# A delta-rule attention block between two expert layers: five stages woven group by group in lockstep, or over all groups by due times

## The chip, the core and the metric

The kernel runs on one core of a Trainium2 chip, as one launch. The metric is device microseconds of that core. TensorE (PE) multiplies, VectorE (DVE), ScalarE (ACT) and GpSimd (POOL) do the elementwise work, SyncE (SP) issues the plain transfers, POOL the gathers and scatters.

## The reference

The input is `x`, 4 sequences of 2048 tokens, 256 wide, float32. The block is a macaron: half an expert layer, attention, half an expert layer, each added to `x`.

```python
x = x + 0.5 * ffn(layernorm(x))      # 8 experts, top 2, capacity 1280 tokens each
x = x + attn(layernorm(x))
x = x + 0.5 * ffn(layernorm(x))
# ffn: silu(xg @ wg) * (xg @ wu) @ wd per expert, F = 1024, weighted scatter-add
# attn, 8 heads of 32:
h = rmsnorm(x, ln1_w)
q, k = l2norm(silu(h @ qw)), l2norm(silu(h @ kw));  v = silu(h @ vw)
beta = sigmoid(h @ bw);  g = -exp(A_log) * softplus(h @ aw + dt_bias)
# for every token:  Sg = exp(g) * S;  S = Sg + beta * k (v - k Sg)^T;  o = q S
o = rmsnorm(o, onorm_w) * silu(h @ gw)
x1 = x + 0.5 * (o @ ow)
y = x1 + 0.5 * silu(rmsnorm(x1, ln2_w) @ fcw) @ pw
```

## The kernel before

Three parts follow one another: the first normalisation, routing and the eight experts; attention; routing and the eight experts again. All matmuls of the expert layers and projections are float32, which the profile counts as two passes each.

Attention treats the token recurrence in chunks of C = 32 tokens. One tile holds the same chunk of the B = 4 sequences, 4 x 32 = 128 partitions, so what is done per head and sequence is a 32 x 32 matmul on one quadrant (`by_sequence`, L566). GC = 4 chunks make a group, and there are NG = 16 groups. A group passes through five stages, each a Python generator that yields after every few instructions a pair (time on PE, latency until it can go on) and a flag for small matmuls:

- `stage_load`: fetch the rows `xt`, layer norm statistics.
- `stage_proj`: normalise (`hh`), transpose (`hT`), project to k, q, v and gate (`pp`, 512 wide) and to beta and g (`pb`).
- `stage_prep`: decay factors (`gg`, `gm`, `pe`, `pd`, `eG`, `ed`), norms of k and q, the products of keys and queries (`pgk`), from them the matrix `A` and `KP`; then `X`, the inverse of a unit triangular matrix of 32 x 32 for each head and token block, by 30 steps of two dependent DVE instructions (`tm`, then `X`, L775 and L779); its transpose `XT`; and `pW`, which needs both `XT` and keys multiplied by their decay (`kq` by `eG`, on POOL, L795).
- `stage_chain`: the recurrence over the four chunks: `pc` from `XT` and v, from `WQD` and the state `S`, then, after the transpose `Z`, from `KP` and `Z`; new `S` and output `O` are transposed out by DVE.
- `stage_out`: norm of `O` (`os`, `ro`), transpose, output projection (`ppo`), first residual `x1`, then the feed-forward (`pm_`, `mT`, `py`), the store, the last layer norm `xn` and the router's logits (`pl`).

The order of PE is written out by hand: `weave` takes the stages' generators and emits, at a planned time, the step that is ready and least far along, with turns between small and large matmuls. The other engines' orders are made by the scheduler, from the order of emission and a few priorities (`urgent`). All engines execute their queues in order. In the version before, `weave` is called 20 times; round `it` holds output of group `it`, chain of `it`+1, preparation of `it`+2, projection of `it`+3 and loading of `it`+4, and every step of a round is emitted before any of the next:

```python
stages = ((65, stage_out), (24, stage_chain), (68, stage_prep), (68, stage_proj), (60, stage_load))
for it in range(1 - len(stages), NG):
    weave([(n, stage, it + d) for d, (n, stage) in enumerate(stages) if 0 <= it + d < NG])
```

The pools `p1` to `p6` have as many buffers as their names say; the PSUM pools `pj` (projections), `tpp` (transposes), `mp` (preparation) and `chp` (chain) have two banks each.

Of the kernel before, what the change touches and what calls it, by code (L numbers as in the profile page):

```python
# [9 lines left out]
F32 = mybir.dt.float32  # L10
# [3 lines left out]
ALU = mybir.AluOpType  # L14
# [4 lines left out]
P = 128  # L19
# [15 lines left out]
for _n, _w in (  # L35
    ("ident", P), ("blk", P), ("before", P), ("after", P), ("upto", P),
    ("prior", P), ("total", P), ("iota", P), ("mle", C),
    ("eye", C), ("below", C), ("rev8", E),
):
    _COLS[_n] = (_W, _W + _w)  # L40
    _W += _w
_PLACE = _W
# [6 lines left out]
def constants():  # L49

    p = np.arange(P)
    b, t = p // C, p % C
    same = b[:, None] == b[None, :]
    c = {
        "ident": np.eye(P),
        "blk": same,
        "before": same & (t[:, None] < t[None, :]),
        "after": same & (t[:, None] > t[None, :]),
        "upto": same & (t[:, None] <= t[None, :]),
        "prior": (b[:, None] < b[None, :]) & (t[:, None] == 0),  # L60
        "total": np.broadcast_to(t[:, None] == 0, (P, P)),
        "iota": np.broadcast_to(p[None, :], (P, P)),
        "mle": t[:, None] <= np.arange(C)[None, :],
        "eye": t[:, None] == np.arange(C)[None, :],
        "below": -30000.0 * (t[:, None] > np.arange(C)[None, :]),
        "rev8": np.broadcast_to(E - np.arange(E)[None, :], (P, E)),
    }
    out = np.zeros((P, _FIND + _FINDS), np.float32)
    for n, (lo, hi) in _COLS.items():
        out[:, lo:hi] = c[n]  # L70
    ch = np.arange(_PLACES)[None, :]
    for i, row in enumerate((p[:, None] * _PLACES + ch, b[:, None] * C * _PLACES + C * ch + t[:, None])):
        lo = _PLACE + 2 * i * _PLACES
        out[:, lo : lo + _PLACES] = row // P
        out[:, lo + _PLACES : lo + 2 * _PLACES] = row % P


    k = P // E
    steps = [k << b for b in range(28, -1, -2) for k in range(4)]
    find = (  # L80
        p[:, None] // k == p[None, :] // k, p[:, None] < p[None, :], p[:, None] == k * np.arange(E),
        np.broadcast_to(np.array(steps, np.int32).view(np.float32), (P, _STEPS)),
    )
    out[:, _FIND:] = np.concatenate(find, axis=1)
    return out
# [10 lines left out]
def macaron_kernel(  # L96
# [19 lines left out]
    cst = cpool.tile([P, _W], F32, name="cst")  # L116
    nc.sync.dma_start(out=cst, in_=consts[:, :_W])
    K = {n: cst[:, lo:hi] for n, (lo, hi) in _COLS.items()}
# [4 lines left out]
    nc.vector.tensor_copy(before16, K["before"])  # L123
    nc.vector.tensor_copy(blk16, K["blk"])
    nc.vector.tensor_copy(iota16, K["iota"])
    ident16 = cpool.tile([P, P], BF16, name="ident16")
    below16 = cpool.tile([P, C], BF16, name="below16")
    nc.vector.tensor_copy(ident16, K["ident"])
    nc.vector.tensor_copy(below16, K["below"])

# [377 lines left out]
    def attention(x1_d, logits, xn_d, x2_d):  # L508
# [4 lines left out]
        with ExitStack() as st:  # L513
# [5 lines left out]
            pv = pool("v", 10)  # L519
# [81 lines left out]
            def stage_load(g):  # L601
# [4 lines left out]
                yield 0, 40  # L606
                for c in range(GC):
                    stats(xt, c, mv)
                    yield 0, 4
# [12 lines left out]
            def stage_proj(g):  # L622
# [5 lines left out]
                yield 0, 40  # L628
                for c in range(GC):
                    hh = p2.tile([P, D], F32, tag="hh", name="hh")  # L630
# [4 lines left out]
                    hT = p2.tile([P, 2, P], F32, tag="hT", name="hT")  # L635
# [21 lines left out]
            def stage_prep(g):  # L657
# [109 lines left out]
                for c in range(GC):  # L767
                    nc.gpsimd.tensor_tensor(
                        KP[:, c, :, 1, :], kq[:, c, 0], bc(edc[:, c, :, C - 1], [2], [P, H, C]), ALU.mult
                    )  # L770
                for j in range(1, C - 1):
# [10 lines left out]
                nc.gpsimd.memset(X[:, 0 : C * C : C + 1], 1.0)  # L782
                for c in range(GC):
                    nc.gpsimd.tensor_tensor(
                        WQD[:, c, :, 2, :], bc(K["eye"], [1], [P, H, C]), bc(eG[:, 1, c], [2], [P, H, C]), ALU.mult
                    )
# [6 lines left out]
                for c in range(GC):  # L793
                    for j in range(2):
                        nc.gpsimd.tensor_tensor(kq[:, c, j], kq[:, c, j], bc(eG[:, 0, c], [2], [P, H, HD]), ALU.mult)  # L795
                    nc.vector.transpose(WQD[:, c, :, 1, :], kq[:, c, 1])
                    yield 0, 0.5
# [8 lines left out]
            def stage_chain(g):  # L806
# [3 lines left out]
                O = G["O"] = p2.tile([P, GC, H, HD], F32, tag="O", name="O")  # L810
                os_ = G["os"] = p2.tile([P, GC, H], F32, tag="os", name="os_")
                for c in range(GC):
# [15 lines left out]
                    for f in range(2):  # L828
# [5 lines left out]
                        nc.vector.transpose(O[:, c, f * HH : (f + 1) * HH], pc[f][:, :, 1])  # L834
# [6 lines left out]

            def stage_out(g):
                G = live[g]
                xt, r, nm, O, os_ = (G[n] for n in ("xt", "r", "nm", "O", "os"))

# [8 lines left out]
                x1 = p1.tile([P, GC, D], F32, tag="x1", name="x1")  # L854
                sx = p2.tile([P, GC], F32, tag="sx", name="sx")
                for c in range(GC):
                    shd = [P, H, HD]
                    nc.vector.tensor_tensor(O[:, c], O[:, c], bc(ro[:, c], [2], shd), ALU.mult)
                    oT = p2.tile([P, 2, P], F32, tag="hT", name="oT")
# [5 lines left out]
                    pp = pj.tile([P, D], F32, tag="pj", name="ppo")  # L865
# [8 lines left out]

                nc.vector.tensor_scalar(sx, sx, 1.0 / D, RMS_EPS, ALU.mult, ALU.add)
# [6 lines left out]
                for c0 in range(0, GC, 2):  # L882
                    hT2 = p2.tile([P, 2, 2 * P], F32, tag="hT2", name="hT2")
                    for i in range(2):
                        c = c0 + i
                        hh = p2.tile([P, D], F32, tag="hh2", name="hh2")
# [40 lines left out]
                xn = p1.tile([P, GC, D], F32, tag="x1", name="xn")  # L927
                for c in range(GC):
# [3 lines left out]
                    xnT = p2.tile([P, 2, P], F32, tag="hT", name="xnT")  # L932
# [12 lines left out]
            def weave(streams):  # L945
# [7 lines left out]
                todo = []  # L953
                for n, stage, g in streams:
                    known = plans.get(stage)
                    todo.append([0.0, 0.0, n, stage(g), known, plans.setdefault(stage, []), 0])
                while todo:
                    ready = [t for t in todo if t[0] <= now]
                    if not ready:
                        now = min(t[0] for t in todo)  # L960
                        continue
                    turn = small if now - since < (1.6 if small else 3.2) else not small

                    def rank(t):
                        coming = t[4][t[6]] if t[4] and t[6] < len(t[4]) else (0, 0)
                        return bool(coming[0]) and (len(coming) > 2) != turn, t[1]

                    t = min(ready, key=rank)
                    step = next(t[3], None)
                    if step is None:  # L970
                        todo.remove(t)
                        continue
# [7 lines left out]
                    t[0] = now + step[1]  # L980
                    t[1] += (step[0] + step[1]) / t[2]
# [4 lines left out]
            stages = ((65, stage_out), (24, stage_chain), (68, stage_prep), (68, stage_proj), (60, stage_load))  # L986
            for it in range(1 - len(stages), NG):
                with tc.manual_schedule(engines={mybir.EngineType.PE}):
                    weave([(n, stage, it + d) for d, (n, stage) in enumerate(stages) if 0 <= it + d < NG])
# [57 lines left out]
```

## Time and profile before

| | us |
|---|---|
| median of 3 runs (3786.07 to 3793.11) | 3789.86 |
| the profiled execution | 3772.04 |
| its span | 3770.3 |
| first matmul of attention | 1162.8 |
| start of the first `pW` of group 0, 4, 13, 15 | 1237.6, 1588.7, 2414.0, 2590.0 |
| last logits of attention | 2730.4 |

The profile is one execution. PE's share of busy time counts pipelined matmuls, so it also counts slow ones; the granted clock (1.00 is full) stands beside it. In the timeline a bracket behind a line is the time the engine idled before it, with what released it: "<-DVE O L834" means that DVE's instruction on line 834, which writes `O`, came last; "issue" that nothing in the profile was waited for. In the windows the columns are the length, then for each engine busy time and instructions, then the clock, the share of the DMA engines and GB/s.

### The profile page before, as it was taken

The page shows a single profiled execution, that of the slowest core. Times are in us where ns is not written, and L with a number is a line of the kernel's source. Part 1 is how long each engine was busy: PE and PEld are TensorE (multiplying, and loading weights), DVE is VectorE, ACT ScalarE, POOL GpSimd, SP SyncE. Part 2 cuts the span into 40 slices and gives each one's busy share as a digit, 9 for nine tenths or more (in the row PEclk, how much of TensorE's full clock was granted, in tenths as well). Part 3 has the DMA queues.
Part 4 walks back from the last instruction along what each step waited for, and adds up shares of the span by engine and source line. Part 5 has one row for each costly group of instructions (what it writes and reads, how often), then busy time and mean ns, then how long its engine had stood idle before and what let it go on. Part 6 is the DMA issues. An engine that isn't in the chain of part 4 may idle for free.

```text
span 3770.3 us, 74243 instructions
## 1 busy us (share of the span) xinstructions
PE 3221.2 (85%) x31883; PEld 2262.2 (60%) x31883; DVE 1721.8 (46%) x5216; ACT 854.4 (23%) x1900; POOL 777.8 (21%) x792
## 2 busy tenths in 40 slices
PE   7179998999995588999999999898708999999998
PEld 6146665665663466666677666667504666656666
DVE  6753323211115657666766666665184342221111
ACT  3011111111112233333333333332201111111111
POOL 0033313222211111111121222220003332222211
PEclk6579999999998799999999999998758999999999
DMA  6212211222102000000000000000121222122211
GB/s 244 105 26 56 59 41 31 61 59 59 23 12 68 2 19 19 19 19 19 19 19 19 19 19 19 13 14 13 25 72 26 60 58 53 20 56 62 58 21 14
DMA packets 94873, 152.91 MB, mean 41 GB/s; under 512 B 13257, under 2 KB 77521, under 8 KB 91473
## 3 DMA queue, kind: packets, MB, share of 16 engines
q1 hardware_dynamic: 63824, 106.21, 8.7%
q0 software_dynamic: 30720, 41.96, 6.6%
q8 instruction: 250, 4.10, 0.4%
q14 instruction: 79, 0.64, 0.1%
HBM read 93.09 MB, written 55.05 MB: 39 GB/s over the span
## 4 chain that ended last, share of the span: by engine, by line
PE 76%; DVE 14%; POOL 4%; DMA 3%; issue 2%; ACT 1%; SPq 0%; POOLq 0%; DVEq 0%; ACTq 0%
PE pg L488 15%; PE pu L490 15%; PE po L497 15%; PE pc L566 5%; PE pp L642 5%; PE py L907 5%; PE ppo L867 2%; PE tp L587 2%; DVE oa L451 2%; DVE over L326 2%; POOL kq L795 1%; PE pgk L566 1%; DVE X L779 1%; DVE tm L775 1%; DMA xg<-xn,idx 1%
## 5 line engine op out<-in xcount | busy, mean ns | idle before, releaser
L493 DVE TENSOR_TENSOR hT<-sg,pu 128x512 f32<-128x512 f32 (+1 forms) x384 | 229.4, 599 | 1181.5 <-PE pu L490 1179.6
L488 PE MATMUL pg<-xT,wg_e 128*128 128x512 f32 (+1 forms) x1536 | 637.7, 537 | 0.0
L490 PE MATMUL pu<-xT,wu_e 128*128 128x512 f32 (+1 forms) x1536 | 616.7, 522 | 0.0
L497 PE MATMUL po<-wd_e,hT 128*128 128x256 f32 x2560 | 560.4, 379 | 0.0
L497 PEld LDWEIGHTS po<-wd_e,hT 128*128 128x128 f32 x2560 | 486.4, 190 | 79.8 <-issue 15.3
L488 PEld LDWEIGHTS pg<-xT,wg_e 128*128 128x128 f32 x1536 | 295.4, 196 | 231.2 <-issue 217.1
L490 PEld LDWEIGHTS pu<-xT,wu_e 128*128 128x128 f32 x1536 | 289.4, 191 | 236.1 <-issue 221.9
L492 ACT ACTIVATE sg<-pg 128x512 f32<-128x512 f32 (+1 forms) x384 | 202.0, 526 | 996.3 <-PE pg L488 964.7
L469 POOL DMA_INDIRECT xg<-xn,idx x160 | 248.0, 1550 | 274.7 <-DVE ws L463 183.3
L642 PE MATMUL pp<-wk,hT 128*128 128x512 f32 x512 | 255.3, 618 | 6.7 <-ACT hT L589 6.0
L503 POOL DMA_INDIRECT x_d<-eo,idx x80 | 128.7, 1608 | 636.0 <-ACT eo L502 493.6
L503 POOL DMA_INDIRECT out_dram<-eo,idx x80 | 124.4, 1554 | 637.7 <-ACT eo L502 490.4
L907 PE MATMUL py<-wpj,mT 128*128 128x256 f32 x1024 | 237.4, 380 | 0.0
L907 PEld LDWEIGHTS py<-wpj,mT 128*128 128x128 f32 x1024 | 192.5, 190 | 40.6 <-issue 17.2
L502 ACT ACTIVATE eo<-po,ws 128x256 f32<-128x256 f32 x160 | 75.9, 475 | 542.9 <-PE po L497 542.9
L775 DVE TENSOR_TENSOR tm<-X 128x30 f32<-128x30 f32 (+14 forms) x480 | 157.9, 329 | 10.1
L779 DVE TENSOR_TENSOR X<-X,tm 128x30 f32<-128x30 f32 (+14 forms) x480 | 157.8, 329 | 10.3
L879 POOL TENSOR_TENSOR xt<-xt,x 128x256 f32<-128x256 f32 x64 | 47.2, 738 | 490.0 <-DVE qa L683 376.8
L476 DVE COPY xT<-tpx 128x256 f32<-128x256 f32 x160 | 67.7, 423 | 172.5 <-PE tpx L475 148.1
L451 DVE TENSOR_TENSOR oa<-aM,iota 128x4096 bf16<-128x4096 bf16 x32 | 141.4, 4420 | 4.5 <-PE tpx L475 4.3
L475 PE MATMUL tpx<-cst,xg 128*128 128x128 f32 x320 | 75.0, 322 | 76.1 <-DMA xg<-xn,idx 42.4
L566 PE MATMUL pc<-XT,vg 32*32 32x32 f32 x4096 | 65.4, 211 | 85.4 <-DVE O L834 61.0
(725 smaller groups left out, 4141.0 us busy)
## 6 DMA issues: line engine op xcount, KB each, us to landing
wg_e<-in_L_ffn_wg_dram SPq DMA_DIRECT2D x16, 1024.0 KB, 4.9
wu_e<-in_L_ffn_wu_dram SPq DMA_DIRECT2D x16, 1024.0 KB, 6.6
wd_e<-in_L_ffn_wd_dram SPq DMA_DIRECT2D x16, 1024.0 KB, 5.7
xt_in<-in_L_attn_x_dram SPq DMA_DIRECT2D x8, 1024.0 KB, 7.6
x_d<-xt_in SPq DMA_DIRECT2D x8, 1024.0 KB, 6.4
xn<-in_xn SPq DMA_DIRECT2D x8, 1024.0 KB, 3.9
xt<-x_d SPq DMA_DIRECT2D x64, 128.0 KB, 3.9
out_dram<-xt SPq DMA_DIRECT2D x64, 128.0 KB, 2.3
```

Of the source, the lines that this page charges most:

```text
L451: nc.vector.tensor_tensor(oa, bc(aM[:, e, hf * HC : (hf + 1) * HC], [2], [P, HC, P]), bc(iota16, [1], [P, HC, P]), ALU.is_equal,)
L469: nc.gpsimd.indirect_dma_start(out=xg, out_offset=None, in_=xn_d[:], in_offset=bass.IndirectOffsetOnAxis(ap=idx[:, t : t + 1], axis=0),)
L488: nc.tensor.matmul(pg[:, :n], wg_e[:, k, fs], xT[:, k, cols], start=(k == 0), stop=(k == 1))
L490: nc.tensor.matmul(pu[:, :n], wu_e[:, k, fs], xT[:, k, cols], start=(k == 0), stop=(k == 1))
L492: nc.scalar.activation(sg[:, :n], pg[:, :n], AF.Silu)
L493: nc.vector.tensor_tensor(hT[:, f, :n], sg[:, :n], pu[:, :n], ALU.mult)
L497: nc.tensor.matmul(po, hT[:, f, (t - t0) * P : (t - t0 + 1) * P], wd_e[:, f, :], start=(f == 0), stop=(f == FF // P - 1),)
L503: nc.gpsimd.indirect_dma_start(out=acc[:], out_offset=bass.IndirectOffsetOnAxis(ap=idx[:, t : t + 1], axis=0), in_=eo, in_offset=None, com ...
L566: nc.tensor.matmul(out[q], lhsT[q], rhs[q], start=first, stop=True, skip_group_check=True)
L642: nc.tensor.matmul(pp, hT[:, k, :], wk[:, k, j * 2 * D : (j + 1) * 2 * D], start=(k == 0), stop=(k == 1),)
L775: nc.vector.tensor_tensor(tmv, Xm[:, j + 1 :, j : j + 1].to_broadcast([P, n, j]), Xm[:, j : j + 1, :j].to_broadcast([P, n, j]), ALU.mult,)
L907: nc.tensor.matmul(py, mT[:, f, i * P : (i + 1) * P], wpj[:, f, :], start=(f == 0), stop=(f == FF // P - 1),)
```

## The change

`weave` is called once for all groups. It is given, for each stage, a start in periods, a length, and the stages that must have got far enough ("held", which stands for the buffers). A stage starts its next group as soon as the stage before has finished that group and the held conditions allow; among the steps that are ready, the one with the earliest due time, (group + start) x 78 plus its progress, is emitted. The first part of `stage_out`, from the norm of `O` to `x1` and the sum `sx`, moves to the end of `stage_chain`. In `stage_prep` the decayed keys and queries, the diagonal of `X` and the last third of `WQD` are emitted ahead of the inverse, and the transposes of the decayed queries within it. Buffers: `vg` 12 instead of 10, `hh` and `hT` three each instead of two, `x1` two, `O` and `os` one; `ppo` takes its bank from the transposes' pool. The planned latencies of loading become short. Of the constants, four blocks that are only needed as bfloat16 or not at all no longer stay in memory: the rest is loaded in a second transfer to a pool that is given back.

```diff
-    cst = cpool.tile([P, _W], F32, name="cst")
-    nc.sync.dma_start(out=cst, in_=consts[:, :_W])
+    cst = cpool.tile([P, _KEPT], F32, name="cst")
+    nc.sync.dma_start(out=cst, in_=consts[:, :_KEPT])
...
+    with tc.tile_pool(name="cst_b", bufs=1) as bp:
+        brief = bp.tile([P, _W - _KEPT], F32, name="cst_b")
+        nc.sync.dma_start(out=brief, in_=consts[:, _KEPT:_W])
...
-            pv = pool("v", 10)
+            pv = pool("v", 12)
...
-                yield 0, 40
+                yield 0, 6
                 for c in range(GC):
                     stats(xt, c, mv)
-                    yield 0, 4
+                    yield 0, 1
...
+                nc.gpsimd.memset(X[:, 0 : C * C : C + 1], 1.0)
+                for c in range(GC):
+                    for j in (1, 0):
+                        nc.gpsimd.tensor_tensor(kq[:, c, j], kq[:, c, j], bc(eG[:, 0, c], [2], [P, H, HD]), ALU.mult)
+                for c in range(GC):
+                    nc.gpsimd.tensor_tensor(
+                        WQD[:, c, :, 2, :], bc(K["eye"], [1], [P, H, C]), bc(eG[:, 1, c], [2], [P, H, C]), ALU.mult
+                    )
                 for j in range(1, C - 1):
...
                     if j % 2 == 0:
                         yield 0, 1.4
-                nc.gpsimd.memset(X[:, 0 : C * C : C + 1], 1.0)
-                for c in range(GC):
-                    nc.gpsimd.tensor_tensor(
-                        WQD[:, c, :, 2, :], bc(K["eye"], [1], [P, H, C]), bc(eG[:, 1, c], [2], [P, H, C]), ALU.mult
-                    )
+                    if j % 4 == 0 and j >= C // 2:
+                        c = j // 4 - C // 8
+                        nc.vector.transpose(WQD[:, c, :, 1, :], kq[:, c, 1])
...
                 for c in range(GC):
-                    for j in range(2):
-                        nc.gpsimd.tensor_tensor(kq[:, c, j], kq[:, c, j], bc(eG[:, 0, c], [2], [P, H, HD]), ALU.mult)
-                    nc.vector.transpose(WQD[:, c, :, 1, :], kq[:, c, 1])
-                    yield 0, 0.5
+                    yield 0, 0
                     pW = mp.tile([P, H, C], F32, tag="m", name="pW")
...
                         with urgent():
                             nc.vector.transpose(S, pc[f][:, :, 2])
-                        nc.vector.transpose(O[:, c, f * HH : (f + 1) * HH], pc[f][:, :, 1])
+                            nc.vector.transpose(O[:, c, f * HH : (f + 1) * HH], pc[f][:, :, 1])
...
-            def stage_out(g):
-                G = live[g]
-                xt, r, nm, O, os_ = (G[n] for n in ("xt", "r", "nm", "O", "os"))
...
-                    pp = pj.tile([P, D], F32, tag="pj", name="ppo")
+                    pp = tpp.tile([P, D], F32, tag="tp", name="ppo")
...
                     yield 0.86, 0.3
+            def stage_out(g):
+                G = live[g]
+                xt, x1, sx = (G[n] for n in ("xt", "x1", "sx"))
                 nc.vector.tensor_scalar(sx, sx, 1.0 / D, RMS_EPS, ALU.mult, ALU.add)
...
-            def weave(streams):
+            def weave(stages, period):
...
+                last = len(stages) - 1
+                todo, done = [None] * (last + 1), [-1] * (last + 1)
+                while done[last] < NG - 1:
+                    for i, (begin, n, stage, held) in enumerate(stages):
+                        g = done[i] + 1
+                        if todo[i] or g == NG or (i and done[i - 1] < g):
+                            continue
+                        if all(done[j] >= g - b for j, b in held):
+                            known = plans.get(stage)
+                            todo[i] = [now, 0.0, n, stage(g), known, plans.setdefault(stage, []), 0]
...
+                    def rank(i):
+                        t = todo[i]
                         coming = t[4][t[6]] if t[4] and t[6] < len(t[4]) else (0, 0)
-                        return bool(coming[0]) and (len(coming) > 2) != turn, t[1]
+                        due = (done[i] + 1 + stages[i][0]) * period + t[1]
+                        return bool(coming[0]) and 1 + ((len(coming) > 2) != turn), due
...
-            stages = ((65, stage_out), (24, stage_chain), (68, stage_prep), (68, stage_proj), (60, stage_load))
-            for it in range(1 - len(stages), NG):
-                with tc.manual_schedule(engines={mybir.EngineType.PE}):
-                    weave([(n, stage, it + d) for d, (n, stage) in enumerate(stages) if 0 <= it + d < NG])
+            stages = (
+                (0.0, 60, stage_load, ((4, 5),)),
+                (0.9, 74, stage_proj, ((2, 2), (3, 3))),
+                (1.4, 74, stage_prep, ((3, 2), (4, 4))),
+                (2.95, 66, stage_chain, ((4, 2),)),
+                (3.85, 78, stage_out, ()),
+            )
+            with tc.manual_schedule(engines={mybir.EngineType.PE}):
+                weave(stages, 78)
```

## The prediction

> **What bounds the kernel now.** I read the page first. The mixture of experts is two equal halves (up to 1152 us and from 2731 us), in which the change touches nothing but the loading of constants; attention fills the 1579 us between, slices 13 to 29 of 40, and there PE is at 9 tenths in the middle and lower at both ends.
>
> ```profile
> span 3770.3 us, 74243 instructions
> ...
> PE 3221.2 (85%) x31883; PEld 2262.2 (60%) x31883; DVE 1721.8 (46%) x5216; ACT 854.4 (23%) x1900; POOL 777.8 (21%) x792
> ...
> PE   7179998999995588999999999898708999999998
> ...
> PEclk6579999999998799999999999998758999999999
> ```
>
> Then the windows of one lockstep round (1677 to 1769 us; the columns are length, PE, PEld, DVE, ACT, POOL busy, clock, DMA share, GB/s), and the same round cut where the clock changes.
>
> ```profile
> 1677.13:1769.06 91.93, 84.42 (x1532) 63.92 (x1531) 63.36 (x232) 32.79 (x79) 17.17 (x29) 0.93 0.08 19
> ...
> 1690.00:1702.00 12.00, 10.81 (x272) 9.16 (x272) 6.96 (x27) 4.88 (x14) 0.00 (x0) 0.57 0.01 3
> ...
> 1718.00:1722.00 4.00, 3.42 (x84) 2.55 (x88) 2.07 (x8) 1.57 (x5) 3.54 (x6) 0.57 0.02 4
> ```
>
> The reader is to see that PE is not simply full: 12 us and 4 us run at clock 0.57, which loses 0.43 x 16 = 6.9 us. The timeline of PE gives the idle stretches in front of them, that of DVE the cause of the longer one.
>
> ```profile
> 1691.80 0.48 PE L566 MATMUL pc<-XT,vg 32*32 32x32 f32 x18 [1.19 <-issue]
> ...
> 1718.58 1.07 PE L566 MATMUL pc<-XT,vg 32*32 32x32 f32 x64 [4.14 <-DVE O L834]
> ...
> 1712.08 1.02 DVE L796 STREAM_TRANSPOSE WQD<-kq 128x256 f32<-128x256 f32 x2 [3.87 <-POOL kq L795]
> ...
> 1716.69 1.02 DVE L796 STREAM_TRANSPOSE WQD<-kq 128x256 f32<-128x256 f32 x2 [3.20 <-POOL kq L795]
> ```
>
> DVE waits 7.1 us in its queue for decayed keys from POOL; the chain's S and O transposes stand behind that wait, and PE behind those. All idle time of PE in the round is 7.1 us. So 91.9 - 6.9 - 7.1 = 77.9 us is matmul work at full clock. Summing rows agrees: dense runs give 0.43 us for a pass of `pp`, 0.216 for `py`, `pm`, `ppo`, 0.38 for a pair of transposes, 0.95, 1.45 and 1.13 for the three `pc` sets of a chunk, 1.03 for `pgk`, 0.68 for `pW`; one group sums to 78.1 us. A round could lose at most some 14 us.
>
> The third thing to see is how long the triangular inverse takes from the last `A` to the second half of `XT`, and that `pW` needs it.
>
> ```profile
> 1737.71 0.42 DVE L754 SCALAR_TENSOR_TENSOR A<-pgk,ed 128x256 f32<-128x256 f32 x1 [3.92 <-PE pgk L566]
> ...
> 1766.70 1.07 DVE L790 STREAM_TRANSPOSE XT<-X 128x512 f32<-128x512 f32 x1
> ...
> 1772.77 0.75 PE L566 MATMUL pW<-XT,kq 32*32 32x32 f32 x64
> ```
>
> That is 30.1 us, against 35.1 us of matmul work that PE has in between: PE never waits for it in a full round.
>
> **The change part by part, in a steady round.** Work per group stays: the instruction order of the changed kernel holds as many matmuls on every line. What moves is where they stand.
>
> *Chain and decayed keys.* On PE the chain's four chunks stood within 19.5 us of work and now spread over 43, with `pm`, `py` and `pp` between; on POOL four decayed-q products now stand directly behind `gm` instead of behind identity products and `ed`, so the DVE transposes lose nearly all of the 7.1 us wait. The 4.14 us gap goes, with its 4 us at 0.57 (1.7 us). What is late next: S and O of chunks 0 and 1, because `pc` of the next chunk now follows at once on the banks that they free (4 transposes of 0.3 us on DVE, about 0.9 and 0.35 us), and Z of chunk 0, queued on DVE behind `gg` and a statistics instruction (0.7 us). Sum +2.0 us. The 1.19 us gap, and the 5.2 us that its 12 slow us lose, come in a run of small matmuls that is now broken by `pp`; it may go wholly or stay (0 to 6.4 us); I let it go, since the round at 2410 us lacks it, at clock 0.98 and 88.8 us long.
>
> *Output projection in the chain's stage.* Here is the cost. Between the last `pgk` of a group and its first `pW` PE now has 26.7 us of work (32 passes each of `pm` and `py` 13.8, ten of `pp` 4.3, eight of `ppo` 1.7, `pc` 4.1, five pairs of transposes 1.9, `pb` 0.9) where it had 35.1. DVE has more: `A`, `KP`, the transposes and the 60 inverse instructions are 24.8 us in both, but the company grows from 8.0 to 14.8 us, with S and O transposes, `os`, the Newton steps of `ro`, four `O` by `ro` products (1.68) and two `x1` additions (0.83). Rows sum to 39.6 us against 32.8. The 32.8 took 30.1, so scaling gives 36.3; stepping through the order with the spacings in the rows (a dependent successor starts 0.03 us after the end, an independent one 0.09 before it) gives 29.9 for before and 33.2 now. I take 33.4 with the hand-over, nearer the second since it meets the old row. PE is in order, so the rest of the loop, `pW` to `pgk`, is 78.1 - 26.7 = 51.4 us, and the round cannot be under 51.4 + 33.4 = 84.8. Most of the stall stands ahead of the first transpose of `O`: its product comes 26 us into DVE's run and PE is there after 21.6, a gap of 4.7 us; a gap of 2.2 follows ahead of `pW`. Behind them are queued `py`, the next `pp` and the chain, for which the whole round waits. `ppo` also moves to the transposes' two banks, so the second transpose of `O` waits for the first `x1` addition: 0.5 us. A gap of 4.14 us was followed by 1.7 us lost to the clock, so 4.7 us gets 1.9; the rows bound it by 0 and 5.2.
>
> The Trainium skill, page "TensorE: Matmul & The Clock Gate", section "What's actually happening", says that the clock halves after an idle window of about 3.4 us and needs as long a busy one. By it the 4.7 us gap would lose an estimated 1.7 us and the 2.2 us gap nothing. The row at 1691.80 contradicts it: 1.19 us idle among 32-wide matmuls came with 12 slow us.
>
> *ACT.* The order shows four table loads per group instead of two: 2 x 1.283 us more on an engine that is busy 32.8 of 91.9 us; hidden, except where `hT` or `mT` is due, 0 to 2.6 us; I take 0.7. The page "ScalarE: Activation LUTs", section "What ACT_TABLE_LOAD costs", speaks against interleaving functions of two sets, at 2.66 us a switch with its drain; by it the engine would carry an estimated 5.3 us more, still far from full.
>
> *Queues.* SP issues per group stores and the load of the fifth group ahead, twelve of 0.43 us. The last `xn` comes some 6 us after `pW`; with eight issues and 3.9 us of landing the load is in by 14, and DVE asks at 19. If that cover of 5 us goes, Z and the chain wait behind the statistics instruction. More buffers, the split constants (one more 0.43 us issue, under the first loads) and the moved memset I cost at nothing, 0 to 1 us.
>
> Round: 78.1 + 6.7 + 0.5 + 1.9 + 2.0 + 0.7 = 89.9, say 90, against 91.7 between the `pW` starts at 1588.67 and 2413.95 (nine rounds). Bounds: 85 if the clock stays up, 95.5 if the 12 slow us stay or return.
>
> **The ends.** In intervals between first `pW` of groups, before and now: to group 0, 85.6 and 88 (five loads' statistics). 0 to 1: 77.1 and 87, as 74.5 us of work replace 42, the chain runs nearly alone at 5.9 us a chunk (rows at 1246 to 1252), and the inverse (34.6) is waited for. 1 to 2: 92.1 and 79 (49 us of work, but 35.7 + 37.9 by the inverse, and 5 for gaps and clock). 2 to 3: 89.5 and 88. 3 to 4: 92.4 and 86. 13 to 14: equal. 14 to 15: 87.3 and 83 (46.4 + 30.8 + 6). From group 15 to the end: 141.5 now for 93.4 us of work, because the lockstep runs chain 15 with projection 14, then group 14, then group 15, each end with its waits:
>
> ```profile
> 2623.27 1.11 PE L587 MATMUL tp<-cst,hh 128*128 128x128 f32 x4 [4.47 <-ACT hh L887]
> ...
> 2660.82 0.69 PE L587 MATMUL tp<-cst,xn 128*128 128x128 f32 x2 [4.33 <-ACT xn L929]
> ...
> 2686.27 1.11 PE L587 MATMUL tp<-cst,hh 128*128 128x128 f32 x4 [3.93 <-ACT hh L887]
> ```
>
> The new order puts the feed-forward of group 14 between the chunks of chain 15 and projection 15 among its last logits: 88.9 us of work, the first two gaps mostly filled, also the slow clock of 2660 to 2690 (some 14 us lost); chain 9, last group's waits 5, its half-clock tail 9: 112.
>
> Sum: +2 +10 -13 -1.5 -6.5 -15 +0 -4 -29.5 = -57.5 us. The profiled execution took 3772.0 us (span 3770.3) and would take 3714; the median of the runs is 3789.9, 17.8 above it for reasons the page does not show, so 3732.
>
> **Rivals.** *PE's own pace.* If the inverse fits into 26.7 us of matmul work, rounds are about 80: the nine lose 10 more each and the other intervals some 65 together, 3732 - 155 = 3577. Against it: 24.8 us of that DVE run hang on one another whatever the company. 7%.
>
> *Slower, by the clock.* The second gap (2.2 us, ahead of a run of `pW`, `pl` and transposes) does what the 1.19 us gap did, 12 us at 0.57 each round, 5.2 us. Over 14 rounds that is +73, 3805. It decides from 57.5 / 14 = 4.1 us per round, a round of 94. For it: that row itself, and the same matmuls in the same place. Against: four `pp` now lie between. 13%.
>
> *Nothing left.* Rounds of 93.5 instead of 90 eat what the ends give: within 7.6 us of 3790. 5%.
>
> **How the numbers follow.** My forecast, rounds of 85.5 to 92.5, has 75%: 3668 to 3770. The range takes in the top of "nothing left" and the rival's nearer part, 3665 to 3798. Faster by over 0.2% (7.6 us, about what a measurement of this kernel can tell): 0.82; within: 0.05; slower: 0.13.
>
> **What would show it.** Right: PE's idle ahead of `tp<-cst,O` and `pW`, released by DVE, together 6 to 9 us a round; none of 4 us ahead of `pc<-XT,vg`; DVE's wait for POOL `kq` under 2 us; intervals of `pW` near 90; last logits about 112 us after the last `pW` starts. Wrong: intervals near 80, or above 94 with a clock below 0.9 in the middle slices.

## The result, and the profile after

The changed kernel takes 3789.4 us (median of 12 runs, 3783.2 to 3796.7), the kernel before 3789.5 beside it: a ratio of 1.0005, 95% interval 0.9992 to 1.0018. The forecast was 57 us less. The profiled execution took 3788.5 us, close to its median, while that of before had been 17.8 under its own; so the traces show the end of attention 10.1 us later, where the medians show no difference.

The page after, the lines that answer to those of before:

```profile
span 3786.7 us, 74190 instructions
...
PE 3208.6 (85%) x31883; PEld 2226.5 (59%) x31883; DVE 1706.6 (45%) x5216; ACT 895.8 (24%) x1934; POOL 780.4 (21%) x792
...
PE   6269998999995687888888888888808998999998
...
PEclk9999999999997888999999999998859999999999
```

In the middle PE falls from 9 tenths to 8 with the same instructions. The windows of a round (from one first `pW` to the next), of the 25 us behind a `pW`, and of four stretches in these:

```profile
1704.68:1797.21 92.53, 82.99 (x1531) 60.80 (x1531) 61.82 (x233) 35.05 (x81) 17.20 (x29) 0.94 0.08 19
...
1797.21:1822.21 25.00, 23.42 (x460) 15.71 (x464) 14.44 (x66) 14.18 (x38) 3.79 (x6) 0.80 0.18 45
...
1797.21:1800.60 3.39, 3.39 (x70) 2.19 (x71) 0.56 (x4) 2.23 (x5) 0.00 (x0) 0.52 0.03 5
...
1800.44:1810.68 10.24, 9.12 (x228) 6.51 (x226) 6.88 (x27) 7.02 (x20) 1.45 (x2) 1.00 0.43 104
...
1810.68:1817.51 6.83, 6.37 (x79) 4.22 (x80) 5.58 (x28) 2.13 (x8) 1.21 (x3) 0.50 0.01 2
...
1811.00:1821.00 10.00, 9.54 (x139) 5.81 (x143) 5.48 (x28) 4.38 (x10) 2.33 (x4) 0.67 0.01 2
```

The slow clock is still there, in the 25 us behind `pW`: 25 x 0.20 = 5.0 us a round, of which 3.39 x 0.48 = 1.6 at once and 10 x 0.33 = 3.3 from 14 us on. Cut where it changes, the clock is 1.00 for 10.24 us and 0.50 for 6.83 us, three times and twice 3.41 us: in the attention part of this trace it is full or half, and half for 3.41 us or a multiple of it, so a slow stretch costs 1.7 us or a multiple of that. PE's timeline shows the waits around it, all of the round's that exceed 1 us among them:

```profile
1783.32 1.12 PE L643 MATMUL pp<-wk,hT 128*128 128x512 f32 x2 [1.27 <-DVE xt L918]
...
1788.78 0.44 PE L588 MATMUL tp<-cst,O 128*128 128x128 f32 x2 [2.62 <-DVE O L859]
...
1797.21 1.08 PE L567 MATMUL pW<-XT,kq 32*32 32x32 f32 x64 [2.76 <-DVE r L578]
...
1810.57 0.95 PE L941 MATMUL pl<-rw,xnT 128*128 128x8 f32 x4 [1.12 <-ACT xnT L590]
...
1823.41 0.45 PE L567 MATMUL pc<-XT,vg 32*32 32x32 f32 x32 [0.28 <-DVE vv L615]
```

The 4.14 us ahead of `pc<-XT,vg` are 0.28, and waits ahead of `tp<-cst,O` and `pW` are new, as forecast. On DVE the inverse run that PE waits for:

```profile
1762.76 0.42 DVE L755 SCALAR_TENSOR_TENSOR A<-pgk,ed 128x256 f32<-128x256 f32 x1 [1.77 <-PE pgk L567]
...
1796.02 1.04 DVE L797 STREAM_TRANSPOSE XT<-X 128x512 f32<-128x512 f32 x1
```

At the start of attention PE waits 32.8 us for group 0's inverse (15.5 us in the kernel before); at its end most of the waits are gone:

```profile
1253.31 3.31 PE L567 MATMUL pW<-XT,kq 32*32 32x32 f32 x231 [32.80 <-DVE XT L797]
...
2688.87 0.44 PE L588 MATMUL tp<-cst,xn 128*128 128x128 f32 x2 [0.86 <-ACT xn L933]
...
2696.62 1.12 PE L588 MATMUL tp<-cst,hh 128*128 128x128 f32 x4 [0.66 <-ACT hh L891]
...
2733.23 0.69 PE L588 MATMUL tp<-cst,xn 128*128 128x128 f32 x2 [4.27 <-ACT xn L933]
```

For comparing kernels one row is enough, the window of the nine rounds from the first `pW` of group 4 to that of group 13; before, then after:

```profile
1588.67:2413.95 825.28, 757.41 (x13771) 574.33 (x13771) 569.54 (x2089) 295.33 (x712) 154.48 (x261) 0.93 0.08 20
```

```profile
1612.03:2448.65 836.62, 750.71 (x13771) 548.44 (x13772) 557.90 (x2089) 315.45 (x729) 154.80 (x261) 0.94 0.08 19
```

Length less PE's busy time is idle time; PE's busy time above 78.1 us of work a round is what the slow clock costs. Before: (825.3 - 757.4) / 9 = 7.5 idle and 757.4 / 9 - 78.1 = 6.1 slow. After: 9.5 and 5.3. All runs below are read this way.

### The profile page after: what moved, and what is told of

The parts are those of the page before. It is cut to its first block, busy times and chain, and to the rows that moved or that the text cites. A ratio compares the mean times of both kernels' runs of the same rounds, so it can differ in the third digit from the quotient of the medians.

```text
span 3786.7 us, 74190 instructions
## 1 busy us (share of the span) xinstructions
PE 3208.6 (85%) x31883; PEld 2226.5 (59%) x31883; DVE 1706.6 (45%) x5216; ACT 895.8 (24%) x1934; POOL 780.4 (21%) x792
## 4 chain that ended last, share of the span: by engine, by line
PE 44%; DVE 13%; ACT 1%; DMA 1%; issue 1%; POOL 0%; POOLq 0%; DVEq 0%; ACTq 0%
PE pg L489 7%; PE pu L491 7%; PE po L498 7%; PE pp L643 4%; PE py L911 3%; PE pc L567 3%; DVE tm L784 3%; DVE X L788 2%; PE tp L588 1%; PE pgk L567 1%; PE ppo L868 1%; PE pl L941 1%; DVE oa L452 1%; PE pW L567 1%; DVE over L327 1%
## 5 line engine op out<-in xcount | busy, mean ns | idle before, releaser
L643 PE MATMUL pp<-wk,hT 128*128 128x512 f32 x512 | 288.8, 677 | 20.0 <-DVE xt L918 13.9
L504 POOL DMA_INDIRECT out_dram<-eo,idx x80 | 132.6, 1658 | 636.0 <-ACT eo L503 486.9
L911 PE MATMUL py<-wpj,mT 128*128 128x256 f32 x1024 | 247.3, 385 | 0.6 <-ACT kq L649 0.2
L784 DVE TENSOR_TENSOR tm<-X 128x30 f32<-128x30 f32 (+14 forms) x480 | 167.5, 349 | 7.2
L643 PEld LDWEIGHTS pp<-wk,hT 128*128 128x128 f32 x512 | 98.6, 215 | 89.7 <-issue 50.7
L476 PE MATMUL tpx<-cst,xg 128*128 128x128 f32 x320 | 73.5, 316 | 81.5 <-DMA xg<-xn,idx 44.5
```

Of the source, the lines that this page charges most:

```text
L504: nc.gpsimd.indirect_dma_start(out=acc[:], out_offset=bass.IndirectOffsetOnAxis(ap=idx[:, t : t + 1], axis=0), in_=eo, in_offset=None, com ...
L643: nc.tensor.matmul(pp, hT[:, k, :], wk[:, k, j * 2 * D : (j + 1) * 2 * D], start=(k == 0), stop=(k == 1),)
L784: nc.vector.tensor_tensor(tmv, Xm[:, j + 1 :, j : j + 1].to_broadcast([P, n, j]), Xm[:, j : j + 1, :j].to_broadcast([P, n, j]), ALU.mult,)
L911: nc.tensor.matmul(py, mT[:, f, i * P : (i + 1) * P], wpj[:, f, :], start=(f == 0), stop=(f == FF // P - 1),)
```

## Experiments

All are edits of the changed kernel unless said otherwise; the ratios are to the kernel before on the same chip, with 95% intervals.

**More work planned beside the inverse.**

```diff
-                        yield 0, 1.4
+                        yield 0, 1.8
```

> Edit: the inverse's planned yields are 1.8 instead of 1.4 us; no instruction is added or removed, only TensorE's order changes. By the rows' durations that order now holds 33.5 us of matmul work between a steady group's last pgk and its first pW; the changed kernel's holds 26.7, while VectorE's run from A to the second XT takes 34.3 us there. Theory L (the round is a loop: VectorE's inverse run, then TensorE's work from pW to the last pgk; TensorE's order has too little beside the inverse, waits there, and the waits halve the clock afterwards): the waits ahead of pW (2.8 us) and ahead of tp<-cst,O (2.6 us) mostly go, the half-clock stretch behind them (9.8 us, 4.9 us lost) shrinks to under 5 us, the round falls from 93.0 to 85 to 89 us and the time to some 3725 us (3700 to 3750). Rival A (ScalarE with its 35 us and four table loads a round sets the round): 3780 to 3800. Rival C (the clock falls because of the run of 32-wide matmuls itself, not because of waits): the half-clock stretch stays near 10 us, only the waits go, and the time is 3745 to 3775.

Measured: 1.0028 (1.0018 to 1.0038), 3792 us. A miss. The wait ahead of `pW` did go, but rounds settled only from group 7 on, at 90.4 us: 7.6 idle in other places, and some 4.7 slow. Before that the new order cost more (104, 94 and 103 us from one first `pW` to the next between groups 2 and 5). So the inverse's loop does not close the round alone: with its wait filled, the other waits and the slow clock still make 90.

**Idle matmuls in the wait, and in the stretch behind it.** First eight ahead of `pW`:

```diff
+                    if j == 28:
+                        pf = tpp.tile([P, D], F32, tag="tp", name="pf")
+                        for k in range(8):
+                            nc.tensor.matmul(pf, ident, wo[:, 0, :], start=True, stop=True)
+                        yield 3.44, 0
```

> Edit: the changed kernel with eight matmuls of 128x256 into a tp tile that nobody reads, 3.4 us of added TensorE work a group (55 us in all at the 0.43 us that ppo and py rows show), placed after the inverse's 28th step, shortly ahead of pW in TensorE's order. Theory L: the work falls into the wait for the inverse, 3789 us plus or minus 15; if the clock's fall is a consequence of that wait it is even some us faster, down to 3750. Rival C and every theory by which TensorE is bound by its own work: 3789 + 45 to 60 = 3834 to 3850. Rival A (ScalarE): 3789 plus or minus 10, so this run does not tell A from L.

Measured: 1.0066 (1.0045 to 1.0088), 3804 us, at the edge of theory L's range: the round grew by 0.3 us for 3.4 us of work, the time, by the ratios, by some 23 of the 55 us added. Then the same matmuls spread behind the four `pW` groups, so that the wait stays:

```diff
+                    pf = tpp.tile([P, D], F32, tag="tp", name="pf")
+                    for k in range(2):
+                        nc.tensor.matmul(pf, ident, wo[:, 0, :], start=True, stop=True)
```

> Edit: the changed kernel with the same eight idle 128x256 matmuls a group as the filler run (3.4 us of added TensorE work, 55 us in all), but two behind each of the four pW groups instead of eight ahead of the first; TensorE's order is otherwise that of the changed kernel, and the wait ahead of pW stays. Theory G (the clock halves after the wait, and stays halved until the dense matmuls come back, so dense work inside the stretch of pW, pl and tp shortens the stretch): half clock per round falls, and the round grows by 0 to 1.5 us: 3789 to 3815 us. Rival H (only filling the wait itself helped in the filler run): the round grows by the whole 3.4 us or, at half clock, more: 3835 to 3870 us.

Measured: 1.0033 (1.0021 to 1.0046), 3797 us. Its rounds are 0.5 us shorter than without 3.4 us of added work; the 25 us behind a `pW` and the nine rounds:

```profile
1799.86:1824.86 25.00, 24.48 (x478) 17.38 (x481) 17.14 (x79) 14.27 (x38) 3.90 (x6) 0.93 0.18 44
```

```profile
1615.49:2447.98 832.49, 758.09 (x13915) 561.54 (x13915) 560.50 (x2089) 315.92 (x729) 156.17 (x261) 0.98 0.08 19
```

The clock behind `pW` is 0.93 instead of 0.80: 3.2 us of slow clock gone, and the 1.12 us wait ahead of `pl` is covered. With 81.5 us of work, 8.3 are idle and 2.7 slow. The whole time, by the ratios, is 0.3% above the changed kernel, some 11 of the 55 us added. Theory G holds, and PE's own work is not what sets the round: in the nine rounds work that nobody needs was free. ScalarE is not tested by this; against it speaks the run with the weave undone below, whose rounds are 3.8 us shorter with as many instructions on ACT (729 in nine rounds).

**The inverse first on VectorE** (high priority for its 60 instructions and `XT`).

> Edit: the inverse's multiplies and adds and the XT transposes are given the high priority that A and KP have; TensorE's order stays. On VectorE the run from A of the last chunk to the second XT has 103 instructions instead of 115: one output add, one bn_stats and bn_aggr, two x1 adds and the newton steps of r3 go behind it, about 2.5 us of busy time by their rows, some 2 us of elapsed time. Theory L: each steady round 1.5 to 2.5 us shorter, 3789 - 20 to 35 = 3754 to 3769. Rivals A and C: 3780 to 3800.

Measured: 0.9989 (0.9976 to 1.0003), 3777 us, by the ratios 0.2% under the changed kernel. The inverse run takes 31.4 us, not 34.3, the wait ahead of `pW` is gone, and the round is 91.6, 1.3 us shorter: 7.6 idle, 5.9 slow. The direction is theory L's; the round falls by a little less than the 1.5 to 2.5 us expected, the time, by the ratios, by 6 us instead of 20 to 35.

**Group 1's projection held back.**

```diff
+                        if i == 1 and g == 1 and not (todo[2] and todo[2][6] >= 23):
+                            continue
```

> Edit: the projections of group 1 may not begin before group 0's last pgk stands in TensorE's order. The theory of the first intervals: in the changed kernel they stand ahead of group 0's pgk, VectorE's inverse of group 0 starts 15 us later, and first matmul to first pW takes 87.1 us instead of 74.8; held back, it takes 74 to 77 us, the other intervals stay, and the time is 3789 - 12 = 3777 (3770 to 3785). Rival: the work held back is missing later, the interval from the first to the second pW takes the 12 us back, and the time is 3789 plus or minus 5.

Measured: 0.9989 (0.9976 to 1.0001), 3781 us. First matmul to first `pW` takes 76.5 us instead of 87.1, and nothing is given back. As expected for the intervals; the whole time, by the ratios (0.9989 against 1.0005), falls by some 6 us of the 12, and each ratio is known to about 5 us.

**The decayed keys alone, in the kernel before.**

```diff
+                for c in range(GC):
+                    for j in (1, 0):
+                        nc.gpsimd.tensor_tensor(kq[:, c, j], kq[:, c, j], bc(eG[:, 0, c], [2], [P, H, HD]), ALU.mult)
...
                 for j in range(1, C - 1):
...
-                        nc.gpsimd.tensor_tensor(kq[:, c, j], kq[:, c, j], bc(eG[:, 0, c], [2], [P, H, HD]), ALU.mult)
```

> Edit: the kernel before with the decayed keys alone moved ahead of the inverse (GpSimd's kq multiplies and the WQD transposes); lockstep and output projection stay, and TensorE's order is the same as before. Theory D (the decayed keys remove a wait that really ended last): the 4.1 us of idle ahead of pc<-XT,vg, where TensorE stood behind VectorE's O behind GpSimd's kq, go in every round, and the 1 to 2 us of half clock behind it with them; the round falls from 91.7 to 86 to 87.5 us and the time from 3782-3789 to 3700 to 3730 us. Rival N (what the changed kernel's rounds suggest: another wait, and the half clock in a new place, take it over): round 90 to 92 us, 3765 to 3790 us.

With them move the diagonal of `X`, the last third of `WQD` and the transposes of the decayed queries. Measured: 0.9836 (0.9801 to 0.9870), 3712 us (six executions, 3705 to 3738), in theory D's range. The nine rounds:

```profile
1570.75:2353.33 782.58, 734.43 (x13771) 556.80 (x13770) 593.64 (x2089) 296.02 (x712) 153.49 (x261) 0.96 0.08 21
```

Rounds of 86.95 us, 5.3 idle and 3.5 slow. The 4.14 us ahead of `pc<-XT,vg` are gone in all nine, but about half of them come back ahead of `pc<-KP`, also in all nine:

```profile
2133.34 0.65 PE L566 MATMUL pc<-KP,Z 32*32 32x64 f32 x32 [2.25 <-DVE Z L829]
```

So the idle time falls by 2.2 us, not by 4.1, and the slow clock by 2.6, more than the 1 to 2 expected. DVE's wait for the keys between 1615 and 2353 us, some eight rounds (total, times, longest), before and here:

```profile
DVE WQD L796 <- POOL kq L795: 56.6, 16, 3.9
```

```profile
DVE WQD L792 <- POOL kq L774: 13.6, 16, 0.9
```

**The decayed keys taken out of the changed kernel.**

> Edit: the changed kernel with the decayed keys back behind the inverse; weave and output projection stay. Theory L: GpSimd's memset, WQD and first kq multiply, 0.16 + 4 x 0.62 + 0.62 = 3.2 us, and what VectorE's WQD transposes add then stand between the inverse and the first pW, and pW waits that much longer: rounds 3 to 5 us longer, 3789 + 48 to 80 = 3835 to 3870 us. Rival N (nothing of the decayed keys was on the path that counts): 3780 to 3800 us.

Measured: 1.0039 (1.0024 to 1.0055), 3801 us: by the ratios 0.3% above the changed kernel, nearer to the rival's answer. DVE waits for the keys again in this order, but the 4.14 us ahead of `pc<-XT,vg` do not return: PE's longest wait there is 0.8 us in eight of the nine rounds, 2.0 us in one:

```profile
DVE WQD L797 <- POOL kq L796: 33.1, 16, 3.4
```

Rounds are 92.8 us. In the weave the decayed keys save next to nothing.

**The output projection back in the output's stage.**

> Edit: the changed kernel with the output projection back in the output's stage; weave and decayed keys stay. Theory L (VectorE's run from A to XT closes the round, and the output projection's company lengthens it; behind it the tp<-cst,O wait of 2.6 us stands inside that stretch): without that company the run takes 27 to 30 instead of 34.3 us, the wait ahead of tp<-cst,O leaves the stretch, steady rounds take 87 to 90 us, and the end is 25 to 35 us longer again: 3760 to 3795 us. Rival W (the weave itself costs what was lost): rounds 92 to 94 us as now, the end 25 to 35 us longer: 3810 to 3830 us.

Measured: 1.0293 (1.0265 to 1.0321), 3897 us. Both theories miss. Rounds are 95.6 us on average, the end 192 us, and PE waits longer ahead of `pW`, not shorter:

```profile
2186.83 1.07 PE L567 MATMUL pW<-XT,kq 32*32 32x32 f32 x63 [5.35 <-DVE nw L577]
```

Under the weave the projection's place in the chain's stage is worth 2.9% (1.0293 against 1.0005), with the stages' starts and lengths left as they were planned for that place; others were not tried.

**The logits later.**

```diff
-                    yield 0.25, 1
+                    yield 0.25, 3
```

> Edit: the planned step between the transposes of xn and the logits matmul pl is 3 us instead of 1. TensorE's order then has pl two to four groups of work behind its transposes, and the four pW groups of 32-wide matmuls stand among output-projection and projection matmuls instead of following one another with pl. Theory C (what the first call left: the clock halves where 32-wide matmuls and waits of about 1 us follow one another, whatever made the wait before pW; rounds of 90 to 92 us without the pW wait show it): the pl waits (1.12 and 0.46 us) go, the half clock per round falls from about 5 to under 2.5 us, rounds take 88 to 90 us, 3730 to 3760 us. Theory L in its strict form (the inverse closes the loop): the wait ahead of pW grows by what pl gives up, 3780 to 3798 us. Rival (the clock falls at intervals of its own): waits alone go, 3765 to 3780 us.

Measured: 1.0093 (1.0069 to 1.0118), 3818 us, worse than every answer. The `pl` waits went, but `pc`, `pp` and `pd` got new ones, and the wait ahead of `pW` grew to a fixed 4.64 us, with a lower clock behind it:

```profile
2171.01 1.08 PE L567 MATMUL pW<-XT,kq 32*32 32x32 f32 x64 [4.64 <-DVE XT L797]
```

```profile
2171.01:2196.01 25.00, 23.07 (x327) 16.71 (x327) 9.30 (x44) 11.20 (x35) 2.90 (x4) 0.72 0.18 44
```

**The weave alone undone.** `weave`, its call and the planned latencies of loading as before; the rest as changed.

```diff
+            stages = ((52, stage_out), (41, stage_chain), (68, stage_prep), (68, stage_proj), (60, stage_load))
+            for it in range(1 - len(stages), NG):
+                with tc.manual_schedule(engines={mybir.EngineType.PE}):
+                    weave([(n, stage, it + d) for d, (n, stage) in enumerate(stages) if 0 <= it + d < NG])
```

> Edit: the changed kernel with the weave alone undone: group by group in lockstep with the planned yields of the kernel before (chain's weight 41 and output's 52, since the output projection's 14.6 us of plan are in the chain's stage); decayed keys, output projection in the chain's stage and the pools stay. By the rows' durations TensorE's order then ends a steady group's chain 39 us after its first pW (changed kernel 66), has the output projection 53 to 71 us after it (75 to 86) and 34.3 us of work between the last pgk and pW (26.7). VectorE's run from A to XT has 115 instructions as in the changed kernel (95 with the decayed keys alone). Theory W (the weave spreads the chain over the round, puts O's scaling and the output projection into the inverse's stretch and leaves TensorE too little beside it): steady rounds 85 to 88 us as with the decayed keys alone (86.95), first matmul to first pW 71 to 75 us, the end 110 to 120 us instead of 143: 3712 - 25 = 3665 to 3700 us. Rival O (the output projection in the chain's stage is at fault, by its company in the inverse's run): rounds of 90 to 93 us, the end 110 to 120 us: 3730 to 3770 us.

> Edit: as the run with the weave undone, but with weights 30 for the chain and 60 for the output, so that the chain ends 37 us after pW and the output projection stands 58 to 81 us after it, again close to the inverse; 35.5 us of work between pgk and pW. Theory W as above: what counts is that TensorE has over 34 us beside the inverse and that O's scaling is done by then; rounds within 1 us of the other run's. Rival O: with the output projection's adds deeper in the inverse's run, rounds 1 to 3 us longer than the other run's.

Measured: 0.9882 (0.9861 to 0.9902), 3739 us, and 0.9946 (0.9933 to 0.9959), 3763 us, with the other weights. The first, nine rounds:

```profile
1596.28:2398.86 802.58, 724.56 (x13772) 547.07 (x13771) 563.71 (x2089) 324.69 (x729) 156.18 (x261) 0.98 0.08 20
```

Rounds of 89.2 us, 8.7 idle, 2.4 slow; the end takes 115.0 us instead of 143. The time is in rival O's range, the round just under it, and both are partly right. Against the decayed keys alone, the output projection in the chain's stage (with the buffers, weights and priorities that go with it) costs 2.2 us a round and gives 28 at the end; the weave costs 3.8 a round more. Rival O's reason is not shown: PE does not wait ahead of the first `pW`, and its longest wait of a round, 2.3 us, is ahead of `py` for DVE's `xt`. The second run (rounds of 92.5, 3.4 us longer) goes rival O's way, but again not for its reason: DVE's inverse run is no longer than in the first (32.2 to 33.8 us a round, there 33.1 to 34.3), and the new wait is 3.6 us ahead of `tp<-cst,xn`, for ACT.

**The decayed keys, with the output projection moved only at the end.** For the last group alone, then for the last two:

```diff
+                if g >= NG - 2:
+                    yield from out_proj(g)
...
+                if g < NG - 2:
+                    yield from out_proj(g)
```

> Edit: the kernel before with the decayed keys ahead, and the output projection moved into the chain's stage for the last group alone (x1 and xn in two buffers, so that group 15's x1 need not wait for group 14's). Rounds as with the decayed keys alone (mean 86.95 us). The end from the last group's first pW to the last pl took 143.1 us there, and 115.0 and 112.8 us where the output projection of the last group ran beside the group before's output stage. If that place alone makes the end short: 3712 - 15 to 28 = 3684 to 3697 us. Rival (the end was short because group 14's own output projection was out of the way too): the end stays above 135 us, 3700 to 3715 us.

Measured: 0.9789 (0.9763 to 0.9814), 3708 us, which is in the rival's range; the end is 131.8 us, between the two answers.

> Edit: as the run with the last group's output projection moved, but for the last two groups (14 and 15), the output's weight 52 for them; rounds up to group 13 as with the decayed keys alone. The last-group run left two readings of its 131.8 us from the last pW to the last pl: theory E2 (group 14's output projection in the last chain's iteration is the rest of what the run with the weave undone saves, 115.0 us): the end falls to 113 to 120 us, the two intervals before it grow by 2 to 8 us together, and the time is 3708 - 8 to 16 = 3692 to 3700 us. Rival E1 (the late order of the last group alone, an unlucky wait of 5 us ahead of tp<-cst,O, makes the 131.8): the end stays at 125 us or more, 3703 to 3715 us.

Measured: 0.9770 (0.9752 to 0.9788), 3710 us beside 3796 for before. The end:

```profile
2532.50:2650.50 118.00, 103.02 (x1321) 85.32 (x1320) 28.96 (x114) 33.78 (x87) 2.90 (x4) 0.85 0.10 24
```

118 us, as theory E2 says, with 10.4 more in the two intervals before than in the last-group run, where 2 to 8 were expected. It is the fastest version found; it beats both kernels by 2.3%. From the last-group run it cannot be told apart.

## Why the prediction failed, point by point

| | before | predicted | measured |
|---|---|---|---|
| idle per round | 7.5 | 9.9 | 9.5 |
| slow clock per round | 6.1 | 1.9 | 5.3 |
| inverse run on DVE | 30.1 | 33.4 | 34.3 |
| a round | 91.7 | 90 | 93.0 |
| group 0's first `pW`, against before | | +2 | +15.7 |
| then 0 to 1, 1 to 2, 2 to 3, 3 to 4 | | +10 -13 -1.5 -6.5 | +15.8 -4.6 +6.5 -9.9 |
| nine rounds | | -15 | +11.3 |
| 13 to 14, 14 to 15 | | 0 -4 | +3.2 +0.8 |
| 15 to the end | | -29.5 | -28.6 |
| sum, to the last logits | | -57.5 | +10.1 |

*Right:* the wait that goes, the two waits that come and their place, the inverse's run, and the gain at the end. The idle time is right as a sum, in part by luck: ahead of `tp<-cst,O` and `pW` it is 5.4 us (the forecast was 6.7, and 6 to 9 was to be the sign), in the chain 0.8 instead of 2.0, while 1.3 us ahead of `pp` and 1.6 ahead of `pl` make up for it. (For the kernel before, the prediction read 7.1 us of idle time a round; the window's row gives 7.5.)

*The term that failed in the steady round is the clock's.* "A gap of 4.14 us was followed by 1.7 us lost to the clock, so 4.7 us gets 1.9": measured are 5.3, and that alone takes the round from 90 to 93, 27 us in nine rounds. The step that fails is to price one gap by its length. The 1.7 us were one stretch of 3.41 us at half clock; the changed kernel has three of these in most rounds, 3 x 1.7 = 5.1 us. The gap ahead of `pW` has about the forecast price, 1.6 us. Missing in the sum is the second stretch, 3.3 us, which begins at the waits of 1.12 and 0.46 us ahead of `pl`. The prediction had such waits in ACT's 0.7 us and gave them no clock, although it had the row at 1691.80, where 1.19 us among short matmuls came with 12 slow us; it let that go because new `pp` passes would break the run. They do not break it where `pl` stands. The run with matmuls behind `pW` covers the longer of these waits, and its 25 us lose 25 x 0.07 = 1.75 us, about the first stretch alone. The prediction had the mechanism as the rival "slower, by the clock": its 5.2 us extra a round were 3.4, and they stand 14 us behind the gap that it blamed. The outcome is that of the rival "nothing left", which had 5%: rounds of 93.0 eat what the end gives.

Shown is that the second stretch is there and that it goes when dense matmuls stand in its place. Whether the waits or the short matmuls bring it is not shown, since no run took the waits alone away. The wait does not fix the price by itself: in the run with idle matmuls ahead of `pW`, 1.11 us ahead of `pl` stand at the same place in every round, and the 25 us behind `pW` lose 3.4, 1.7 and 0 us in three successive rounds; the three windows, and the wait in the first and the third:

```profile
1707.45:1732.45 25.00, 22.79 (x569) 16.17 (x568) 18.14 (x82) 12.79 (x35) 4.09 (x7) 0.86 0.18 45
...
1801.69:1826.69 25.00, 22.13 (x572) 15.70 (x572) 18.32 (x82) 13.35 (x37) 4.09 (x7) 0.93 0.17 45
...
1895.69:1920.69 25.00, 21.42 (x575) 14.83 (x575) 18.08 (x82) 14.13 (x37) 4.09 (x7) 1.00 0.18 46
```

```profile
1719.29 1.02 PE L946 MATMUL pl<-rw,xnT 128*128 128x8 f32 x4 [1.11 <-ACT xnT L590]
...
1907.53 0.61 PE L946 MATMUL pl<-rw,xnT 128*128 128x8 f32 x4 [1.11 <-ACT xnT L590]
```

*The other half is the start.* The prediction counted only the loads' statistics up to group 0's first `pW`. In the changed order group 1's projections stand ahead of group 0's last `pgk`, which ends at 1220.5 us instead of 1205, and DVE's inverse starts that much later; 3.4 us of this lie ahead of attention, whose first matmul starts at 1166.2 us instead of 1162.8. Holding them back removes 10.6 us. The four intervals after it are 19 us above the forecast together. PE is busy for 293 us of them in both kernels, so the 7.7 us that they have more than before are idle time; where the rest of the forecast went stays open.

*What the sum hid.* The change was costed as a whole. Apart, the decayed keys are worth -1.6% with the lockstep, while without them the changed kernel is only 0.3% slower: in the weave PE no longer stands behind that wait, so two of the parts remove the same one. The weave costs 1.2% (1.0005 against 0.9882), the output projection's place, with what goes with it, 0.5% in the lockstep (0.9882 against 0.9836). Together the three make about zero. What is shown is the parts' size and that dense work buys the clock back; which rule of the due times makes the weave's order worse by 3.8 us a round (2.9 of it slow clock) was not tried apart.

The Trainium skill, page "TensorE: Matmul & The Clock Gate", section "What's actually happening", says that the clock follows a free-running window of about 3.4 us, falls after an idle one and needs a busy one to rise. The runs agree with the free-running part: behind the same `pW`, with the same matmuls, the run with idle matmuls ahead of `pW` shows clocks of 0.86, 0.93 and 1.00 in three successive rounds, again and again (the windows above). They do not agree that it takes an idle window of that length: the changed kernel's longest wait in a round is 2.8 us, and its clock falls all the same.

## What to carry to other kernels

Cost each part of a bundled change by itself, against the order that the other parts leave: two parts that remove the same wait gain once, and the cheapest part alone may beat the bundle. Price a wait on TensorE with the matmuls around it: one of 1 us among short matmuls cost three times its length in clock in one round and nothing in another, and 3.4 us of dense matmuls a round, some 1.4% of the time, added only 0.3% where they stood among the short ones. Read the first and last groups' order as closely as the steady one.

## What had not been expected of the hardware

Adding 3.4 us of useless dense matmuls to each round made the round 0.5 us shorter: the granted clock over the nine rounds rose from 0.94 to 0.98. (The whole kernel, by the ratios, is 0.3% longer.) A wait of 1.12 us among short matmuls was followed by 10 us at a clock of 0.67, dense `pp` passes among them, while 2.76 us ahead of `pW` cost 3.4 us at 0.52.

In four runs the rounds came to stand at whole multiples of 3.41 us: 85.3 us between groups 4 and 8 with the last two output projections moved (25.0 times), 88.8 between 5 and 13 with the weave undone (26.0), 92.2 between 4 and 8 with idle matmuls behind `pW` (27.0), 95.5 between 8 and 13 with the logits later (28.0). The changed kernel's rounds, 92.4 to 94.0, do not stand still in this way. If the clock holds rounds to such steps, a saved wait need not shorten a round by its own length; no run tests that.
